# Graph products of a stack of graph-network layers: from 64 x 128 blocks of weights to 64 x 64 blocks on TensorE

## The chip, the cores and the metric

The kernel runs on one core of one Trainium2 chip. The metric is the device time of one launch in microseconds (us), as the median of several runs. A profile is one execution of the same program with the hardware profiler on; its rows name the engines PE (TensorE's matmuls), PEld (TensorE's weight loads), DVE (VectorE), ACT (ScalarE), POOL (GpSimd) and SP (SyncE, which here issues most DMAs).

## The reference

The input is `x`, 128 graphs of 64 nodes with 256 features, and one 64 x 64 adjacency matrix `adj`. Everything is fp32. Four layers follow each other; between them the stack adds the layer's input back and normalizes. Cut to what matters here:

```python
# layer 0: x <- LN(x + L0(x, adj))
agg = einsum('nm,bmd->bnd', A_hat, features)          # graph product
h   = relu(batchnorm(agg @ W1.T + b1)); out = batchnorm(h @ W2.T + b2)
# layer 1: a Laplacian product, then masked attention and an MLP
xp  = einsum('mn,bnf->bmf', L_norm, x)                # graph product
x1  = relu(layernorm(xp @ Wc + bc)) + x
q, k, v = x1 @ Wq, x1 @ Wk, x1 @ Wv                   # 4 heads of 64
o   = softmax(where(adj > 0, q k^T / 8, -1e9)) v
x2  = layernorm(x1 + o @ Wo); x = layernorm(x2 + gelu(x2 @ W1 + b1) @ W2 + b2)
# layer 2: two graph convolutions, then LSTMs over windows of 1, 2, 3 and 4 nodes
h = relu(einsum('ts,bsh->bth', adj, x @ Wg0 + bg0))   # graph product
h = relu(einsum('ts,bsh->bth', adj, h @ Wg1 + bg1))   # graph product
for p in (1, 2, 3, 4): h[last node of each window of p] = lstm_last(h windows)
# layer 3: attention with additive scores over the graph
out = softmax(mask(leaky_relu(Wh a1 + (Wh a2)^T))) Wh
```

So there are four graph products of a 64 x 64 matrix with the 64 nodes of each graph: one in layer 0, one in layer 1, two in layer 2.

## The kernel before

**Tiling.** The 128 graphs are cut into 16 blocks of 8. A block in "token-major" form is a tile of 128 partitions: partition = two graphs of 64 nodes, and beside it `NT` = 4 such pairs `t` with 256 features each. The two partition halves are `halves = slice(0, 64), slice(64, 128)`, one graph in each. In "feature-major" form the partition is one of 128 features, and the tile has two feature halves `c` with 512 tokens each.

**The graph product.** `aggregate(ps, y, mT)` (L333 to L346; its matmuls are profiled at L340) multiplies the graphs of a block with a 64 x 64 matrix that lies twice on the diagonal of `mT`. It takes the block itself as weights, so that the result comes out feature-major and needs no transpose. For each feature half `c` (2), pair `t` (4) and partition half `s` (2) there is one matmul with weights of 64 rows x 128 columns (`y[h, t, c * P : (c + 1) * P]`) and a moving operand of 64 rows x 64 columns (`mT[h, h]`). That is 16 matmuls a block, each of which the profile shows as two loads and two matmul instructions. The results for the two partition halves go to different halves of the PSUM buffer (`part(ps, s, g)`), and the copy that empties it puts them back side by side (`joined`, `runs`).

It is called for layer 0 in `first_block` (matrix `AhT`, emptied by VectorE at L574), for layer 1 in `block` (`LnT`, emptied by ScalarE at L765) and twice for layer 2 in `gcn_block` (`bdAT`, emptied by ScalarE at L1323 and L1342): 4 x 16 = 64 products.

**Neighbours on TensorE.** `to_fm` (L354) and `to_tm` (L361) transpose between the two forms with 64-row pieces, 16 to a block; the attention weights are transposed in the same way at L870. The scores of layer 1 (L836) and attention times values (L884) are matmuls of 64 x 64 weights on a 64 x 64 moving operand, 32 to a block. Full-array products with weights are `mm_fm` (L367), `mm_tm` (L379), the LSTM's (L1062, L1134, L1271, L1273), the MLP's second product (L945), and those of the second half of layer 0 (L642).

**What sets the order.** The program's order is written by a planner in the kernel itself. Every task (a block of a layer, an LSTM unit) is a generator that yields `step(engine, us, ps=..., sl=...)`: the engine of the next piece, the planner's cost for it in us, and how many PSUM buffers and SBUF tiles it takes or gives back. `flow` keeps one list of running tasks and always issues the step that can begin soonest by its own clock (with 2 us of head start for TensorE steps, `MARGIN`); there are four PSUM buffers (`PS`) and eight tiles and more that are lent later (`mem`). Each engine then executes its own queue strictly in the order issued. The costs hence change no instruction, but they decide the order on all queues, and with it which buffer a step gets and when a DMA is issued on SP.

The first `flow` runs layer 0: `first_block` for all blocks beside the chain `eig` (26 squarings of a 128 x 128 matrix for the Laplacian's largest eigenvalue, L499), then the batch norm's coefficients, then `second_block`. The second `flow` runs everything else as streams: `end_block` and `block` of layer 1, `gcn_block` of layer 2 with the first LSTM, the LSTM units of 2, 3 and 4 nodes (`unit`), and `last_block` for layer 3.

Of the kernel before, what the change touches and what calls it, by code (L numbers as in the profile page):

```python
# [15 lines left out]
P = 128  # L16
B, N, D = 128, 64, 256
NBLK = 16
TB = 512
NT = 4  # L20
# [13 lines left out]
def kernel(ctx: ExitStack, tc: tile.TileContext, a: dict, out: bass.AP):  # L34
    nc = tc.nc
    V, S, G, T = nc.vector, nc.scalar, nc.gpsimd, nc.tensor
# [206 lines left out]
    halves = slice(0, N), slice(N, P)  # L243
    for s in range(2):
        h = halves[s]
# [71 lines left out]

    def part(ps, s, g):  # L320

        return ps[:, s * TB + g * N : s * TB + (g + 1) * N]

    def joined(ps, n=2 * NT):

        return ps.rearrange("p (s g e) -> p g s e", s=2, e=N)[:, :n]

    def runs(ap):

        if len(ap.shape) == 2:  # L330
            return ap.rearrange("p (g s e) -> p g s e", s=2, e=N)
        return ap.rearrange("p t (c s e) -> p (t c) s e", s=2, e=N)

    def aggregate(ps, y, mT):


        for c in range(2):
            for t in range(NT):
                for s, h in enumerate(halves):
                    T.matmul(  # L340
                        part(ps, s, c * NT + t),
                        y[h, t, c * P : (c + 1) * P],
                        mT[h, h],
                        start=True,
                        stop=True,
                    )  # L346

    def to_fm(ps, y):

# [13 lines left out]
    def mm_fm(ps, w, yT, nk, off=0):  # L363

        for c in range(2):
            for k in range(nk):
                T.matmul(  # L367
                    ps[:, c, :],
                    w[:, k, (off + c) * P : (off + c + 1) * P],
                    yT[:, k, :],  # L370
                    start=(k == 0),
                    stop=(k == nk - 1),
                )
# [34 lines left out]
    with c0:  # L408
# [151 lines left out]
        def first_block(i):  # L560
            if i >= len(early):
                yield step("Q", 6.0, sl=1)
                xs = mem.take()
                nc.sync.dma_start(tm(mem[xs]), x_blk[i])
            else:
                xs = early[i]
            yield step("T", 0.95, ps=1, sl=1)
            ps = PS.take()
            ag = mem.take()
            aggregate(PS[ps], tm(mem[xs]), AhT)  # L570
            mem.give(xs)
            yield step("V", 1.25, ps=-1)
            aggT = fm(mem[ag])
            V.tensor_copy(runs(mem[ag]), joined(PS[ps]))  # L574
            PS.give(ps)
            for hf in range(2):
                dst = fm(Xs[i]) if hf == 0 else H[i]
                yield step("T", 3.45, ps=1)
                ps = PS.take()
                mm_fm(fm(PS[ps]), W1T, aggT, 2, off=2 * hf)  # L580
                if hf:
                    mem.give(ag)
                yield step("S", 1.3, ps=-1, waits=hf == 1)
                for c in range(2):
                    f = 2 * hf + c
                    S.activation(dst[:, c, :], fm(PS[ps])[:, c, :], AF.Identity, bias=cols["b1"][:, f : f + 1])
                PS.give(ps)
                yield step("V", 1.25, waits=hf == 1)
                for c in range(2):
                    V.bn_stats(st1[:, 2 * hf + c, i, :], dst[:, c, :])  # L590
            mark("l0a", i)
# [144 lines left out]
    def end_block(i):  # L736
        x = X[i]
        yield step("Q", 6.0, sl=1)
        xin = mem.take()
        nc.sync.dma_start(tm(mem[xin]), x_blk[i])  # L740
        yield step("S", 1.4)
        for c in range(2):
            S.activation(
                H[i][:, c, :], H[i][:, c, :], AF.Identity, scale=sc2[:, c : c + 1], bias=sh2[:, c : c + 1]
            )
        yield step("T", 0.5, ps=1)
        ps = PS.take()
        to_tm(PS[ps], H[i])
        mark("h", i)
        yield step("V", 1.25, ps=-1)  # L750
        V.tensor_tensor(runs(x), joined(PS[ps]), runs(mem[xin]), ALU.add)
        PS.give(ps)
        mem.give(xin)
        yield from ln_steps_act(x)
        mark("end", i)

    def block(i):
        x = X[i]
        mark("begun", i)
        yield step("T", 0.95, ps=1, sl=1)  # L760
        ps = PS.take()
        s_xp = mem.take()
        aggregate(PS[ps], x, LnT)
# [4 lines left out]
        ps = PS.take()  # L768
# [4 lines left out]
        y = tm(mem[s_y])  # L773
# [3 lines left out]
        yield step("V", 1.25)  # L777
        V.scalar_tensor_tensor(y, y, 0.0, x, ALU.max, ALU.add)

        yield step("T", 0.5, ps=1, sl=1)  # L780
        ps = PS.take()
        s_x1 = mem.take()
        to_fm(PS[ps], y)
# [5 lines left out]
        for w in (Wq, Wk):  # L789
            yield step("T", 3.45, ps=1, sl=1)  # L790
            ps = PS.take()
# [12 lines left out]
        ps = PS.take()  # L804
        s_v = mem.take()
        pv = PS[ps].rearrange("p (b u e) -> p b u e", b=8, u=2)
        for b in range(8):
            for r in range(2):
                for k in range(2):
# [4 lines left out]
                        start=(k == 0),  # L814
                        stop=(k == 1),
# [8 lines left out]
        G.tensor_tensor(y, y, row["bo"], ALU.add)  # L824


        yield step("T", 1.8, ps=1, sl=1)
        ps = PS.take()
        s_e = mem.take()
        pq = PS[ps].rearrange("p (r g m) -> p r g m", r=2, g=8)  # L830
        for t in range(NT):
            for u in range(2):
                for s in range(2):
                    b = 2 * t + s
                    for r in range(2):
# [4 lines left out]
                            start=True,  # L840
                            stop=True,
# [20 lines left out]
        G.tensor_tensor(em, em, bc_last(sums, N), ALU.mult)  # L862


        yield step("T", 0.5, ps=1, sl=1)
        ps = PS.take()
        s_a = mem.take()
        for g in range(8):
# [4 lines left out]
        aT = mem[s_a].rearrange("p (g m) -> p g m", g=8)  # L873
        S.copy(runs(mem[s_a]), joined(PS[ps]))
        PS.give(ps)
        yield step("T", 1.3, ps=1, sl=1)
        ps = PS.take()
        s_o = mem.take()
        po = fm(PS[ps])
        for b in range(8):  # L880
            t, s = b // 2, b % 2
            for u in range(2):
                for r in range(2):
# [4 lines left out]
                        start=True,  # L888
                        stop=True,
# [7 lines left out]
        ps = PS.take()  # L897
# [5 lines left out]
        yield from ln_steps(y)  # L903


        yield step("T", 0.5, ps=1, sl=1)
        ps = PS.take()
        s_x2 = mem.take()
        to_fm(PS[ps], y)
# [15 lines left out]
        for hf in range(2):  # L925
            yield step("T", 3.45, ps=1, sl=1)
            ps = PS.take()
# [5 lines left out]
            for c in range(2):  # L933
                f = 2 * hf + c
# [7 lines left out]
        ps = PS.take()  # L942
        for t in range(NT):
            for k in range(4):
# [4 lines left out]
                    start=(k == 0),  # L949
                    stop=(k == 3),  # L950
# [360 lines left out]
        mem.give(s_cell)  # L1311

    def gcn_block(i):
        yield step("T", 0.95, ps=1, sl=1)
        ps = PS.take()
        s_a = mem.take()
        aggregate(PS[ps], X[i], bdAT)
        yield step("Q", 4.0, waits=False)
        nc.sync.dma_start(XD[i], X[i])
        mem.add([Xs[i]], Clock.end, part=("x", i // 2) if i < 8 else None)  # L1320
        mark("x", i)
        yield step("S", 1.05, ps=-1)
        S.copy(runs(mem[s_a]), joined(PS[ps]))  # L1323
        PS.give(ps)
        yield step("T", 3.45, ps=1, sl=1)
        ps = PS.take()
        s_h1 = mem.take()
        mm_tm(tm(PS[ps]), fm(mem[s_a]), Wg0, 2)
        mem.give(s_a)
        yield step("V", 1.25, ps=-1)  # L1330
        h1 = tm(mem[s_h1])
        V.tensor_tensor(h1, tm(PS[ps]), bc_mid(rb0, NT), ALU.add)
        PS.give(ps)
        yield step("S", 1.05)
        S.activation(mem[s_h1], mem[s_h1], AF.Relu)
        yield step("T", 0.95, ps=1, sl=1)
        ps = PS.take()
        s_a = mem.take()
        aggregate(PS[ps], h1, bdAT)
        mem.give(s_h1)  # L1340
        yield step("S", 1.05, ps=-1)
        S.copy(runs(mem[s_a]), joined(PS[ps]))  # L1342
        PS.give(ps)
        yield step("T", 3.45, ps=1, sl=1)
        ps = PS.take()
        s_h2 = mem.take()
        mm_fm(fm(PS[ps]), Wg1, fm(mem[s_a]), 2)
        mem.give(s_a)
# [24 lines left out]
        mark("p", 1, i)  # L1373
# [89 lines left out]
    def last_block(i, t0=0, nt=NT):  # L1463
# [5 lines left out]
        r = nt / NT  # L1469
# [3 lines left out]
        for c in range(2):  # L1473
# [1 line left out]
                hb[:, c, :].rearrange("p (b n) -> p b n", n=N),  # L1475
                hT_block(i)[:, c, :, 2 * t0 : 2 * (t0 + nt)].rearrange("p n b -> p b n"),
            )
        yield step("T", 0.5 * r, ps=1)
        ps = PS.take()
        to_tm(PS[ps], hb)  # L1480
        mem.give(s_h)
# [3 lines left out]
        PS.give(ps)  # L1485
        yield from ln_steps_act(x)

        yield step("T", 0.5 * r, ps=1, sl=1)
        ps = PS.take()
        s_xT = mem.take()  # L1490
        to_fm(PS[ps], x)
# [11 lines left out]
        for t in range(0, nt, 2):  # L1503
            end = t == nt - 2
            yield step("T", 1.75, ps=1, sl=int(t == 0))
            ps = PS.take()
# [4 lines left out]
            for j in range(2):  # L1511
                for k in range(2):
# [4 lines left out]
                        start=(k == 0),  # L1517
                        stop=(k == 1),
# [16 lines left out]
        ps = PS.take()  # L1535
# [19 lines left out]
        ps = PS.take()  # L1555
# [8 lines left out]
        ps = PS.take()  # L1564
        po = PS[ps].rearrange("p (e u d) -> p e u d", e=2, u=2)
        for t in range(0, nt, 2):
            for j in range(2):
                for h in range(2):
# [4 lines left out]
                        start=True,  # L1573
                        stop=True,
# [170 lines left out]
```

## Time and profile before

| | |
|---|---|
| median of 3 runs | 2440.89 us (2439.8 to 2445.77) |
| profiled execution, its time | 2446.48 us |
| profiled execution, its span (first to last instruction) | 2444.7 us |
| mean granted TensorE clock | 0.979 |
| instructions | 38027 |
| DMA | 57.74 MB, 24 GB/s over the span |

How to read the rows: a group's row has the line, engine and operation, what is written and read, the shapes and how often, then busy time, mean ns of one, and the idle time just before it with what ended it. Busy time of a group is the time in which at least one of its instructions ran: instructions overlap, so a mean of 272 ns does not mean that one starts every 272 ns. For the pace of a run of matmuls the timeline is used, from the start of one row to the start of the next. A timeline row has start, length, engine, line, operation and count. Weights are shown as rows*columns ahead of the moving shape: `64*128 64x64` is 64 x 128 weights and 64 columns that move.

### The profile page before, as it was taken

To read this page: it belongs to the slowest core of one execution; us is meant where nothing else is said; L and a number is where in the kernel's file an instruction comes from. 1 tells how busy PE (TensorE), PEld (TensorE's weight loads), DVE (VectorE), ACT (ScalarE), POOL (GpSimd) and SP (SyncE) were. 2 spreads that over 40 slices of the span, in tenths; PEclk is the share of its full clock that TensorE was granted. 3 is DMA by queue.
4 is the path that set the end of the run, shared out by engine and by line. 5 is a ranking of instruction groups with operands and counts; after the bars stand their busy time and mean duration, and the time that the engine had idled before them with its cause. 6 is when DMAs were issued, how large, how long until landed. Compare 5 with 4: busy or idle time off the path is not lost. (4 is left out here: it accounts for less than half of the span.)

```text
span 2444.7 us, 38027 instructions
## 1 busy us (share of the span) xinstructions
PE 2323.0 (95%) x15636; PEld 1789.4 (73%) x15636; DVE 1255.6 (51%) x2904; ACT 1185.4 (48%) x2168; POOL 591.0 (24%) x441
## 2 busy tenths in 40 slices
PE   8999878999999999999999999999999999989997
PEld 5548655767666667566677888899999888877775
DVE  4557577656447538266334344344444445455445
ACT  1248553444444343444444444444445554567676
POOL 0002134323224223233222222222221222122112
PEclk9999889999999999999999999999999999999998
DMA  5100301100000000001000000000001000101101
GB/s 154 52 1 1 106 26 40 36 9 10 1 10 10 18 10 10 1 18 44 9 27 1 27 18 1 1 18 1 1 1 35 1 10 9 35 27 44 52 18 53
DMA packets 42622, 57.74 MB, mean 24 GB/s; under 512 B 6224, under 2 KB 35536, under 8 KB 42448
## 3 DMA queue, kind: packets, MB, share of 16 engines
q1 hardware_dynamic: 41344, 54.22, 6.8%
q8 instruction: 123, 2.02, 0.4%
q10 hardware_dynamic: 1104, 1.08, 0.1%
q14 instruction: 51, 0.42, 0.1%
HBM read 38.52 MB, written 16.78 MB: 23 GB/s over the span
## 5 line engine op out<-in xcount | busy, mean ns | idle before, releaser
L1134 PE MATMUL ps<-x,x 128*128 128x256 f32 x864 | 212.9, 381 | 1.6 <-DVE x L1193 1.0
L1134 PEld LDWEIGHTS ps<-x,x 128*128 128x128 f32 x864 | 160.6, 190 | 25.2 <-issue 2.0
L1134 PE MATMUL ps<-t,x 128*128 128x256 f32 x704 | 170.0, 380 | 0.0
L314 ACT ACTIVATE x<-x,ln_nm,ln_rs 128x256 f32<-128x256 f32 x188 | 99.6, 592 | 122.9 <-DVE ln_nm L311 122.9
L1134 PEld LDWEIGHTS ps<-t,x 128*128 128x128 f32 x704 | 132.9, 190 | 18.9 <-issue 0.8
L308 POOL TENSOR_TENSOR ln_rs<-ln_rs,neghalf 128x4 f32<-128x4 f32 (+1 forms) x72 | 69.9, 970 | 213.0 <-DVE ln_rs L274 200.7
L367 PE MATMUL ps<-t,W1T 128*128 128x512 f32 x256 | 116.5, 603 | 0.0
L1210 ACT ACTIVATE t<-t,bih 128x512 f32<-128x512 f32 (+2 forms) x63 | 40.4, 641 | 105.7 <-DVE t L1200 101.0
L294 POOL TENSOR_TENSOR ln_rs<-ln_rs,neghalf 128x4 f32<-128x4 f32 x32 | 36.6, 1143 | 224.4 <-DVE ln_rs L274 224.4
L1062 PE MATMUL ps<-h,wL 128*128 128x192 f32 (+2 forms) x456 | 90.4, 352 | 0.0
L1062 PE MATMUL ps<-h,x 128*128 128x256 f32 x384 | 86.8, 380 | 1.5 <-ACT t L1074 1.5
L1193 DVE COPY t<-ps 128x256 f32<-128x256 f32 (+2 forms) x63 | 23.4, 371 | 123.9 <-PE ps L1134 123.9
L272 DVE BATCH_NORM_STATS2 ln_st<-x 128x6 f32<-128x256 f32 x224 | 85.4, 403 | 0.4
L367 PEld LDWEIGHTS ps<-t,W1T 128*128 128x128 f32 x256 | 47.4, 194 | 49.4 <-issue 49.4
L1062 PEld LDWEIGHTS ps<-h,wL 128*128 128x128 f32 x456 | 70.1, 190 | 16.8 <-issue 15.8
L1062 PEld LDWEIGHTS ps<-h,x 128*128 128x128 f32 x384 | 72.7, 190 | 12.3 <-ACT t L1074 1.6
L1074 ACT ACTIVATE t<-ps,bih 128x512 f32<-128x512 f32 (+3 forms) x108 | 63.6, 639 | 34.3 <-PE ps L1062 34.2
L1062 PE MATMUL ps<-t,wL 128*128 128x512 f32 x168 | 73.7, 594 | 1.3 <-ACT t L1360 0.7
L1074 ACT ACTIVATE x<-ps,bih 128x512 f32<-128x512 f32 (+3 forms) x84 | 48.9, 634 | 52.3 <-PE ps L1062 52.1
L273 DVE BATCH_NORM_AGGREGATE ln_mv<-ln_st 128x2 f32<-128x6 f32 x448 | 71.6, 167 | 0.0
L1210 ACT ACTIVATE x<-x,bih 128x512 f32<-128x512 f32 (+2 forms) x64 | 41.8, 653 | 57.6 <-DVE x L1200 57.4
L1062 PE MATMUL ps<-x,wL 128*128 128x512 f32 x144 | 62.9, 593 | 0.0
(712 smaller groups left out, 5760.6 us busy)
## 6 DMA issues: line engine op xcount, KB each, us to landing
t<-in_x_dram SPq DMA_DIRECT2D x26, 512.0 KB, 4.2
xd<-x SPq DMA_DIRECT2D x16, 512.0 KB, 2.6
x<-xd SPq DMA_DIRECT2D x6, 512.0 KB, 3.4
out_dram<-x SPq DMA_DIRECT2D x6, 512.0 KB, 3.0
h<-in_x_dram SPq DMA_DIRECT2D x5, 512.0 KB, 3.9
wL<-in_L_gnn_Wih_dram SPq DMA_DIRECT2D x2, 1024.0 KB, 5.1
x<-in_L_gnn_Whh_dram SPq DMA_DIRECT2D x2, 1024.0 KB, 6.2
t<-xd SPq DMA_DIRECT2D x4, 512.0 KB, 3.6
```

What stands on the lines that cost most here:

```text
L272: V.bn_stats(st[:, t, :], y[:, t, :])
L273: V.bn_aggr(mv[:, t, :], st[:, t, :])
L294: G.tensor_tensor(rs, rs, neghalf[:, :NT], ALU.pow)
L308: G.tensor_tensor(rs, rs, neghalf[:, :n], ALU.pow)
L314: S.activation(y[:, t, :], y[:, t, :], AF.Identity, scale=rs[:, t : t + 1], bias=nm[:, t : t + 1])
L367: T.matmul(ps[:, c, :], w[:, k, (off + c) * P : (off + c + 1) * P], yT[:, k, :], start=(k == 0), stop=(k == nk - 1),)
L1062: T.matmul(spread(fm(PS[ps])[:, j, :n], q), WL[p][0][:, k, m], x_of(0, q)[:, k], start=(k == 0), stop=(k == 1),)
L1074: S.activation(of(sl)[:, j], fm(PS[ps])[:, j, :n], AF.Tanh if g == 2 else AF.Sigmoid, bias=bias(g, c))
L1134: T.matmul(dst, WS[p][name](k, g), y[:, k], start=first and k == 0, stop=k == 1, skip_group_check=not first)
L1193: V.tensor_copy(y[:, 1, :], v[:, 0, :])
L1210: S.activation(of(act[g])[:, 0], of(act[g])[:, 0], f, bias=bias(g, 0))
```

## The change

`aggregate` splits each weight block of 128 feature columns in two of 64 (`f`), and writes each to its own half of the output partitions (`[to]`). A block then takes 32 matmuls of 64 x 64 weights in the place of 16 of 64 x 128. The loop runs over the two column halves and, inside, over the two partition halves, so that four matmuls in a row use the four different quarters of the array. What is computed, where it lands and who empties it stay as they were. Beside that, the planner's costs of TensorE steps are rewritten: products, transposes, scores, attention times values, and the transposes of the last blocks. Line numbers after it stand two higher.

```diff
         for c in range(2):
             for t in range(NT):
-                for s, h in enumerate(halves):
-                    T.matmul(
-                        part(ps, s, c * NT + t),
-                        y[h, t, c * P : (c + 1) * P],
-                        mT[h, h],
-                        start=True,
-                        stop=True,
-                    )
+                for f, to in enumerate(halves):
+                    for s, h in enumerate(halves):
+                        T.matmul(
+                            part(ps, s, c * NT + t)[to],
+                            y[h, t, c * P + f * N : c * P + (f + 1) * N],
+                            mT[h, h],
+                            start=True,
+                            stop=True,
+                        )
...
# first_block, block, gcn_block (twice): ahead of aggregate
-            yield step("T", 0.95, ps=1, sl=1)
+            yield step("T", 1.15, ps=1, sl=1)
...
# end_block: to_tm; block: to_fm (twice) and the transposes of the attention weights
-        yield step("T", 0.5, ps=1)
+        yield step("T", 0.65, ps=1)
...
# block: scores
-        yield step("T", 1.8, ps=1, sl=1)
+        yield step("T", 1.15, ps=1, sl=1)
...
# block: attention times values
-        yield step("T", 1.3, ps=1, sl=1)
+        yield step("T", 1.15, ps=1, sl=1)
...
# last_block: to_tm and to_fm, r = 1 for a whole block and 0.5 for half of one
-        yield step("T", 0.5 * r, ps=1)
+        yield step("T", 0.2 + 0.45 * r, ps=1)
```

More of the change, by code (lines that the diff above doesn't have):

```diff
@@ L759, in block @@
         mark("begun", i)
-        yield step("T", 0.95, ps=1, sl=1)
+        yield step("T", 1.15, ps=1, sl=1)
         ps = PS.take()
@@ L778, in block @@
         V.scalar_tensor_tensor(y, y, 0.0, x, ALU.max, ALU.add)
-        yield step("T", 0.5, ps=1, sl=1)
+        yield step("T", 0.65, ps=1, sl=1)
         ps = PS.take()
@@ L862, in block @@
         G.tensor_tensor(em, em, bc_last(sums, N), ALU.mult)
-        yield step("T", 0.5, ps=1, sl=1)
+        yield step("T", 0.65, ps=1, sl=1)
         ps = PS.take()
@@ L875, in block @@
         PS.give(ps)
-        yield step("T", 1.3, ps=1, sl=1)
+        yield step("T", 1.15, ps=1, sl=1)
         ps = PS.take()
@@ L903, in block @@
         yield from ln_steps(y)
-        yield step("T", 0.5, ps=1, sl=1)
+        yield step("T", 0.65, ps=1, sl=1)
         ps = PS.take()
@@ L1313, in gcn_block @@
     def gcn_block(i):
-        yield step("T", 0.95, ps=1, sl=1)
+        yield step("T", 1.15, ps=1, sl=1)
         ps = PS.take()
@@ L1335, in gcn_block @@
         S.activation(mem[s_h1], mem[s_h1], AF.Relu)
-        yield step("T", 0.95, ps=1, sl=1)
+        yield step("T", 1.15, ps=1, sl=1)
         ps = PS.take()
@@ L1486, in last_block @@
         yield from ln_steps_act(x)
-        yield step("T", 0.5 * r, ps=1, sl=1)
+        yield step("T", 0.2 + 0.45 * r, ps=1, sl=1)
         ps = PS.take()
```

## Prediction

> **What bounds the kernel now.** I read the page first: busy shares, then the forty slices.
>
> ```profile
> PE 2323.0 (95%) x15636; PEld 1789.4 (73%) x15636; DVE 1255.6 (51%) x2904; ACT 1185.4 (48%) x2168; POOL 591.0 (24%) x441
> PE   8999878999999999999999999999999999989997
> PEclk9999889999999999999999999999999999999998
> ```
>
> TensorE is busy 2323 of 2444.7 us and every other compute engine is near half. A mean over stages proves little, so next comes the table of busy time in six stretches that I cut where the kind of work changes: first blocks, second blocks, ramp of layer 1, layer 1 with the graph layer, LSTM, end. Columns: stretch, length, PE, PEld, DVE, ACT, POOL busy, clock, DMA.
>
> ```profile
> 0.00:140.00 140.00, 131.96 (x781) 82.29 (x782) 69.05 (x144) 31.63 (x49) 2.51 (x15) 1.00 0.32 90
> 140.00:260.00 120.00, 113.53 (x436) 82.40 (x435) 76.48 (x136) 81.45 (x144) 22.60 (x16) 0.97 0.02 5
> 260.00:430.00 170.00, 139.81 (x1275) 101.46 (x1274) 118.36 (x307) 88.03 (x132) 54.38 (x39) 0.87 0.19 58
> 430.00:1400.00 970.00, 941.68 (x7157) 648.25 (x7156) 504.34 (x1102) 421.28 (x567) 280.15 (x173) 0.99 0.04 15
> 1400.00:2000.00 600.00, 595.30 (x3375) 540.37 (x3374) 268.74 (x544) 285.60 (x649) 139.79 (x105) 1.00 0.03 9
> 2000.00:2445.00 445.00, 400.75 (x2620) 334.59 (x2618) 218.64 (x673) 277.42 (x630) 91.61 (x94) 0.97 0.10 33
> ```
>
> PE is the bound in every stretch but two: the ramp (30 us idle) and the end (44 us idle). From 430 to 1400 it idles 28 us in 970, and in the first 140 us only 8, of which 7.5 pass before its first matmul. So PE time taken out there moves the end, unless something new holds PE up.
>
> Where are the products that change? The same table for L340 alone (PE, PEld):
>
> ```profile
> 0.00:140.00 140.00, 35.72 (x512) 34.24 (x512) 1.00 0.32 90
> 260.00:430.00 170.00, 11.35 (x128) 10.94 (x128) 0.87 0.19 58
> 430.00:1400.00 970.00, 86.74 (x1408) 81.55 (x1408) 0.99 0.04 15
> ```
>
> 2048 instructions, 64 products of 32 (each fp32 matmul is two), 16 in the first stretch, 4 in the ramp, 44 in the long PE-bound one. PEld is as busy as PE: each load of 64 x 128 weights serves a moving operand of only 64 columns.
>
> **The change part by part.** *The product itself.* Its price is read from start to next start in the timeline of PE, since the printed length holds a tail that overlaps the next row:
>
> ```profile
> 456.53 2.00 PE L340 MATMUL ps<-bdAT,t 64*128 64x64 f32 x32
> 458.36 1.95 PE L340 MATMUL ps<-bdAT,x 64*128 64x64 f32 x32
> 460.15 1.95 PE L340 MATMUL ps<-LnT,x 64*128 64x64 f32 x32
> 462.03 2.41 PE L367 MATMUL ps<-x,Wg 128*128 128x512 f32 x5
> ```
>
> 1.79 to 1.83 us when a product of the same form follows, 1.88 before a full-array one (1.93 at 1379.40). For the new form the kernel already holds a twin: the scores at L836 are 32 fp32 matmuls, so 64 instructions, of 64 x 64 weights on a moving 64 x 64, in the same order of quarters (both row halves for one column half, then the other), the row halves to different halves of the PSUM buffer.
>
> ```profile
> 330.10 1.16 PE L836 MATMUL ps<-h,t 64*64 64x64 f32 x64 [0.40 <-ACT h L820]
> 331.19 0.71 PE L354 MATMUL ps<-ident,t 64*128 64x64 f32 x15
> ...
> 1115.19 1.16 PE L836 MATMUL ps<-x,x 64*64 64x64 f32 x64
> 1116.17 1.11 PE L884 MATMUL ps<-t,t 64*64 64x64 f32 x64
> 1117.21 2.00 PE L340 MATMUL ps<-bdAT,t 64*128 64x64 f32 x32
> ```
>
> 1.09 us before another form, 0.98 before its own: 0.11 is the price of changing the array's form behind it. The built order of the changed kernel has 51 of the 64 products followed by another form (41 before, because the transposes had the old form), so about 1.08 us on average against 1.87: **0.79 us less each**. Before the product, 48 enter from another form against 46: nothing.
>
> The Trainium skill speaks against this: "TensorE: Matmul & The Clock Gate", in the section "Wait — 56ns, not 53.3ns?", says that matmul starts never come closer than about 25 ns, however small the matmul. Twice as many instructions would then take 64 x 25 = 1.6 us, saving 0.27 each and 17 us in all. The row gives 1.09 us for 64, or 17 ns a start, under that floor; the row decides. A skill-based sum would be 2424.
>
> *Clock.* Five products ran at about half pace: three between 9.32 and 20.68 (3.5 us each) and two at 289 to 296 (3.6), where the granted clock reads 0.50. At half pace the new form should take twice 1.08, so 1.4 less each. The first three are only worth half: L367's matmuls go from 0.86 to 0.43 us apart at about 25 us, and if that moment stays put, slow work fills the gap. Sum: 59 x 0.79 = 46.6; three at 0.7 = 2.1; two at 1.4 = 2.8; together **51.5 us of PE**.
>
> *What of it lies beside other work.* In the ramp PE waits for LN and copies, and I strike half of the two warm products there: -0.8. In the 970 us the other engines' work is squeezed into 935, and waits of PE that were hidden come out: between 0 and a doubling of the 28 us idle; I take 3, as DVE goes only from 52% to 54%. In the first stretch each product is copied out by DVE in 1.22 us (L574), more than the new 1.08; a run of products then goes at DVE's pace, but at most three stand together and buffers lie between: -0.3.
>
> *The step costs.* The change also rewrites what the planner thinks of steps: products 0.95 to 1.15, transposes 0.5 to 0.65, scores 1.8 to 1.15, attention times values 1.3 to 1.15, and the same for the last blocks. These issue nothing. But the planner writes every queue's order from them, so all five queues are reordered (SP's loads and stores too: layer-3 reads and output stores change places). Instruction counts are equal apart from the products and ACT's table loads, 78 before, 68 after: 10 x 1.28 us of ACT, half of them among layer 1's gelu and exp, where ACT is 43% busy and hides them; at most 2 us reach PE. The new costs stand closer to the rows (1.15 for 1.09, where 0.95 stood for 1.87), which should not hurt. No row prices an order; I bound it by the places where PE idles and could idle less or more: about a third of the 102 us idle in ramp, long stretch and end, so -30 to +30, and take 0, since the order's shape at the end is nearly the same: behind the last LSTM matmul of L1134 stands about 154 us of PE work (151 before), priced by shape. DMA is busy 3 to 10% after 430 us, and hides any moved transfer; without that cover a 512 KB read costs 3.4 us.
>
> Sum: 51.5 - 0.8 - 3 - 0.3 = 47.4, and about 0.5 for the table loads: **48 us**. The profiled execution took 2446.5 us (span 2444.7), so 2398.5; it was 5.6 above the median of the runs, 2440.9, so the median to expect is **2393**.
>
> **The rivals.**
>
> *A, the waits shrink too.* Better costs give a better order; a third of the 102 us is won: 2393 - 25 = about 2368 to 2378. For: before, 64 products were planned at half their length, so PE ran late against the plan. Against: of the 28 us idle, the named waits are single events of 1 to 3.5 us.
>
> *B, evacuation takes over.* "TensorEngine Tiling (Array Packing)", section "PSUM Bottleneck", says tiling quickens TensorE but not the emptying of PSUM. ACT's copy behind a product takes 1.01 us (L765, L1323), DVE's 1.22; neither shrinks. If every product had its copy exposed by a third, 64 x 0.35 = 22 back: 2415. Against: ACT waited for these copies, not the reverse (L1323 15.7 and 13.7 us for L340), and four PSUM buffers with other streams' matmuls lie between.
>
> *C, slower: the end comes apart.* From 2000 us PE already idles 44 of 445 us waiting for ACT and DVE in LSTM gates and last blocks. If the new order puts the last LSTM units so late that last blocks stand alone behind them, PE idle there grows. It decides once the added idle passes 48 + 7 = 55 us, more than a doubling: say 70 added, 2463. Against: the 154 against 151 us above.
>
> *D, the quarters don't run side by side.* One matmul after another at the old 57 ns would make 64 x 57 = 3.65 us a product and cost 64 x 1.8 = 114 us: 2555; break-even is at 29 ns a start. The twin at 17 ns nearly excludes it; the only difference is that two quarters here read the same moving operand.
>
> **How the numbers follow.** The forecast has 0.66, A 0.16, B 0.13, C 0.04, D 0.01. The forecast's own range is 2380 to 2406 (half of the order's and waits' bounds). The range for 8 in 10 takes in most of A and B: 2371 to 2412. A measurement tells about 0.3%, 7 us, from no change. Faster than that: forecast, A and nearly all of B, 0.94; within it, B's far end, 0.02; slower, C and D with some room for an order that I can't price, 0.04.
>
> **What would show it.** Right: L342 (the moved L340) with 4096 PE instructions and about 75 us busy against 134; the product from start to next start 0.98 to 1.10 us; PE busy near 2270; idle in 430 to about 1365 at 25 to 35 us; the end of the graph-layer stretch some 45 us earlier. Wrong: 25 ns a start (the skill's floor) or more; L574 or the ACT copies in the list of PE's waits with over 10 us; more than 70 us idle in the last 445 us (C); PE idle in the long stretch doubled.

## The result and the profile after

The changed kernel takes 2427.91 us (median of four runs, 2427.06 to 2429.18) against 2440.35 us for the kernel before on the same chip: a ratio of 0.9945, 95% interval 0.9928 to 0.9962. That is faster, by 12.4 us or half a per cent. The forecast said 48, and its wider range, for 8 in 10, ended at 2412.

The page of the changed kernel: busy time, then the forty slices of PE and its clock.

```profile
PE 2278.0 (94%) x17684; PEld 1741.2 (72%) x17684; DVE 1257.5 (52%) x2904; ACT 1174.4 (48%) x2158; POOL 592.9 (24%) x441
PE   7999798989999999999999999999999999998995
PEclk9999798999999999999999999999999999999997
```

PE is busy 45.0 us less (2323.0 before), but the span, 2425.5, is only 19.2 shorter than the 2444.7 of before, whose profiled run was 5.6 above its own median. The rest is idle time of PE: 2425.5 - 2278.0 = 147.5 us against 121.7. The same six stretches as before show where. Columns: stretch, length, PE, PEld, DVE, ACT, POOL busy, clock, DMA.

```profile
0.00:140.00 140.00, 126.33 (x1319) 69.75 (x1320) 72.15 (x154) 35.47 (x55) 2.52 (x15) 0.98 0.34 91
140.00:260.00 120.00, 113.49 (x461) 86.81 (x459) 76.34 (x134) 80.68 (x145) 22.41 (x16) 0.97 0.05 14
260.00:430.00 170.00, 135.96 (x1454) 95.80 (x1454) 118.32 (x313) 86.05 (x126) 56.09 (x40) 0.86 0.19 55
430.00:1400.00 970.00, 927.33 (x8535) 624.00 (x8534) 516.44 (x1110) 423.11 (x577) 287.42 (x175) 0.98 0.05 16
1400.00:2000.00 600.00, 595.96 (x3424) 546.59 (x3423) 265.28 (x536) 280.64 (x649) 140.80 (x105) 1.00 0.02 7
2000.00:2425.00 425.00, 378.94 (x2499) 318.26 (x2497) 208.99 (x663) 268.44 (x608) 83.67 (x91) 0.95 0.10 34
```

The stretch that held 28 us of PE idle now holds 970 - 927.3 = 42.7; the first holds 13.7 (8.0), the ramp 34.0 (30.2). The LSTM stretch is unchanged, as is the end (46.1 against 44.3).

Was the product itself as cheap as forecast? The same table for its matmuls alone (L342, which was L340), and two places of PE's timeline:

```profile
0.00:140.00 140.00, 18.78 (x1024) 17.28 (x1024) 0.98 0.34 91
260.00:430.00 170.00, 8.80 (x320) 7.22 (x320) 0.86 0.19 55
430.00:1400.00 970.00, 50.85 (x2752) 44.84 (x2752) 0.98 0.05 16
```

```profile
61.31 1.16 PE L342 MATMUL ps<-AhT,t 64*64 64x64 f32 x64
62.40 0.49 PE L501 MATMUL ps<-eM 128*128 128x128 f32 x2
...
98.10 2.09 PE L342 MATMUL ps<-AhT,t 64*64 64x64 f32 x128
100.12 0.49 PE L501 MATMUL ps<-eM 128*128 128x128 f32 x2
```

Yes. Twice the instructions take 78.4 us in all where 133.8 stood. From start to next start a product takes 1.09 us, two in a row 2.02: 16 to 17 ns a matmul on average. So 55 us of TensorE work is gone (54 by 64 products at 0.84 us, below), and the question is who took back 43 of them. The list of PE's waits (columns: waiting line, what it waited for, us in total, times, longest) begins so:

```profile
PE ps L356 <- ACT x L314: 6.8, 1, 6.8
PE ps L501 <- DVE eM L505: 6.7, 2, 6.1
...
PE ps L947 <- ACT t L937: 6.0, 2, 3.2
...
PE ps L369 <- ACT x L788: 4.5, 1, 4.5
PE ps L947 <- ACT x L937: 4.3, 1, 4.3
PE ps L947 <- ACT h L937: 4.0, 1, 4.0
```

Four of the rows left out (PE waiting at L472, L363 and L610, and at L356 for L780: 5.0 to 6.4 us each) stand in the list of before too, as long or longer. No wait is large and few repeat, and no copy behind a product is among the leaders: normalization (L314), gelu (L937), copies ahead of the next projection. There is no one thief, so the experiments separate three suspects: the new order, the chains between the matmuls, and GpSimd.

### The profile page after: what moved, and what is told of

It is laid out like the page before. It is cut to its first block, busy times and chain, and to the rows that moved or that the text cites. A ratio compares the mean times of both kernels' runs of the same rounds, so it can differ in the third digit from the quotient of the medians.

```text
span 2425.5 us, 42138 instructions
## 1 busy us (share of the span) xinstructions
PE 2278.0 (94%) x17684; PEld 1741.2 (72%) x17684; DVE 1257.5 (52%) x2904; ACT 1174.4 (48%) x2158; POOL 592.9 (24%) x441
## 5 line engine op out<-in xcount | busy, mean ns | idle before, releaser
L1136 PE MATMUL ps<-x,x 128*128 128x256 f32 x896 | 220.0, 380 | 0.8 <-DVE x L1204 0.7
L1136 PEld LDWEIGHTS ps<-x,x 128*128 128x128 f32 x896 | 167.0, 190 | 22.2 <-DVE x L1204 0.9
L314 ACT ACTIVATE x<-x,ln_nm,ln_rs 128x256 f32<-128x256 f32 x172 | 91.3, 592 | 121.2 <-DVE ln_nm L311 121.2
L369 PE MATMUL ps<-t,W1T 128*128 128x512 f32 x256 | 117.6, 606 | 0.0
L1064 PE MATMUL ps<-h,wL 128*128 128x192 f32 (+2 forms) x480 | 101.0, 364 | 0.0
L1076 ACT ACTIVATE t<-ps,bih 128x512 f32<-128x512 f32 (+3 forms) x116 | 69.7, 652 | 37.2 <-PE ps L1064 36.9
L369 PEld LDWEIGHTS ps<-t,W1T 128*128 128x128 f32 x256 | 47.5, 194 | 49.5 <-issue 49.4
L1064 PEld LDWEIGHTS ps<-h,x 128*128 128x128 f32 x384 | 72.5, 190 | 11.9 <-DVE h L903 1.3
L272 DVE BATCH_NORM_STATS2 ln_st<-x 128x6 f32<-128x256 f32 x208 | 79.8, 404 | 0.4
L369 PE MATMUL ps<-t,wA 128*128 128x512 f32 x144 | 70.1, 633 | 2.5 <-ACT t L788 2.5
L1136 PE MATMUL ps<-x,wA 128*128 128x192 f32 (+1 forms) x352 | 65.5, 313 | 1.1 <-DVE t L1204 1.1
L1202 DVE TENSOR_TENSOR t<-ps,t 128x512 f32<-128x512 f32 (+2 forms) x61 | 36.7, 602 | 56.0 <-PE ps L1136 47.0
```

Source lines behind the costliest of these rows:

```text
L272: V.bn_stats(st[:, t, :], y[:, t, :])
L314: S.activation(y[:, t, :], y[:, t, :], AF.Identity, scale=rs[:, t : t + 1], bias=nm[:, t : t + 1])
L369: T.matmul(ps[:, c, :], w[:, k, (off + c) * P : (off + c + 1) * P], yT[:, k, :], start=(k == 0), stop=(k == nk - 1),)
L1064: T.matmul(spread(fm(PS[ps])[:, j, :n], q), WL[p][0][:, k, m], x_of(0, q)[:, k], start=(k == 0), stop=(k == 1),)
L1076: S.activation(of(sl)[:, j], fm(PS[ps])[:, j, :n], AF.Tanh if g == 2 else AF.Sigmoid, bias=bias(g, c))
L1136: T.matmul(dst, WS[p][name](k, g), y[:, k], start=first and k == 0, stop=k == 1, skip_group_check=not first)
```

## The experiments

Medians and ratios are against the kernel before, run beside them. "Idle" is the span less PE's busy time.

One thing has to be added to the kernel's description: the built queues are not quite the planner's list. Instructions of one engine can change places (GpSimd runs L434, L436, L435, L437 in e3), and two L361 transposes stand inside a product of before at 294.05 us. "Same order" below is that of the built queues.

**The two halves of the change alone.** First, quarters with all the planner's costs as before; the built order is then the one of before but for a handful of neighbours that changed places (8 of PE's other 13588 instructions, 14 of DVE's 2904, 4 of ACT's 2168):

```diff
# e1: from the changed kernel, all costs put back
-            yield step("T", 1.15, ps=1, sl=1)   # and every other new cost
+            yield step("T", 0.95, ps=1, sl=1)
# e2: from the changed kernel, the product put back
-                for f, to in enumerate(halves):
-                    for s, h in enumerate(halves):
-                        T.matmul(part(ps, s, c * NT + t)[to], y[h, t, c * P + f * N : c * P + (f + 1) * N], ...)
+                for s, h in enumerate(halves):
+                    T.matmul(part(ps, s, c * NT + t), y[h, t, c * P : (c + 1) * P], ...)
```

> The product in quarters, every step cost of the planner as before: the built order of all queues is then that of the kernel before but for a handful of transposes. Theory 'order' (the new costs wrote an order with more idle PE): about 2400 us, the 48 us of the forecast less some 8 us for the stall at the start, where VectorE sits behind the sums of layer 0's second weights; PE idle near 125 us and busy near 2275. Theory 'squeeze' (with less PE work the same chains on ACT, DVE and POOL show, whatever the order): 2422 to 2432 us, PE idle 145 us or more.

> The old product (64 x 128 weights), all new step costs: the order of the changed kernel with the old PE work. Theory 'order': slower than before by about the 25 to 30 us that the changed kernel lacks, 2465 us. Theory 'squeeze': 2441 us within 6, as the longer products cover the chains again.

e1: 2420.08 us, ratio 0.9914 (0.9897 to 0.9931), idle 144.4. e2: 2457.62 us, 1.0074 (1.0055 to 1.0093). So the new costs lose 17 us with the old product and 8 with the new one, and they are the smaller part: with the order kept, the quarters bring 20.7 us, not 54. Both results lie between what the two theories named, e1 just under the range of "squeeze".

Because e1 has before's order, its matmuls can be compared one by one, and the lead (start in before less start in e1) drawn up along the run. It was 10.9 us at 138 us behind 16 products, 17.8 at 436 behind 21, and 26.9 at 1400 behind all 64. Up to 436 us nothing is missing: 21 x 0.84 = 17.6. Behind that it is a staircase. Nearly every product lifts the lead by 0.74 to 0.95 us, typically 0.84, and in between it falls. Summed over the matmuls between 440 and 1420 us, where the interval to the matmul before grew: 17.8 us fell in single intervals above 1.3 us (waits), and 13.1 us in short ones, nearly all runs of matmuls at half pace (L367 at 0.85 us instead of 0.43, L379 at 0.43 instead of 0.22) behind a wait. Against both stand 43 products, 36 us, and 4.7 of other gains, mostly half-pace runs of before that are gone. The granted clock says the same: its mean over this stretch is 0.990 in before and 0.981 in e1 (422 to 1393 us there). (5.6 us of the lead at the end is before's own profiled run above its median.)

Sixteen idle times just before a matmul grew by more than 0.15 us there, by 15.6 us together. 11.9 of it came at ten places where PE of before had already waited, 0.4 to 3.5 us each. A result of ScalarE ended twelve of the sixteen; copies behind a product (L1324, L1343) are 2.0 us of it.

The largest fall, 6.2 us, reads off the timelines of all engines. Before:

```profile
598.23 1.38 DVE L285 TENSOR_SCALAR h<-h,ln_mv,ln_rs 128x256 f32<-128x256 f32 x4 [1.19 <-POOL ln_rs L282]
599.52 1.28 DVE L1352 TENSOR_TENSOR t<-ps,rb 128x512 f32<-128x512 f32 x2
600.60 0.71 PE L354 MATMUL ps<-ident,h 64*128 64x64 f32 x16
...
600.89 1.06 ACT L1360 ACTIVATE t<-t 128x1024 f32<-128x1024 f32 x1 [9.64 <-DVE t L1352]
601.40 2.36 POOL L824 TENSOR_TENSOR h<-h,rows 128x1024 f32<-128x1024 f32 x1 [3.21 <-PE ps L354]
...
602.01 1.55 PE L1062 MATMUL ps<-t,wL 128*128 128x512 f32 x3 [0.70 <-ACT t L1360]
```

And e1, lines one higher:

```profile
576.72 0.71 PE L355 MATMUL ps<-ident,h 64*128 64x64 f32 x16
576.81 3.40 DVE L285 TENSOR_SCALAR h<-h,ln_mv,ln_rs 128x256 f32<-128x256 f32 x4 [1.20 <-POOL ln_rs L282]
577.53 2.54 POOL L825 TENSOR_TENSOR h<-h,rows 128x1024 f32<-128x1024 f32 x1 [0.75 <-PE ps L355]
580.13 1.27 DVE L1353 TENSOR_TENSOR t<-ps,rb 128x512 f32<-128x512 f32 x2
...
581.50 1.06 ACT L1361 ACTIVATE t<-t 128x1024 f32<-128x1024 f32 x1 [14.10 <-DVE t L1353]
...
582.61 1.22 PE L1063 MATMUL ps<-t,wL 128*128 128x512 f32 x1 [5.17 <-ACT t L1361]
```

Follow the bracket of each row backwards. The LSTM's matmul waits for ACT, ACT for DVE's add, and that stands in DVE's queue behind L285, which waited for GpSimd's L282: a chain that the product is not part of, and which the earlier PE only waits on for longer. And a second thing: the transposes came 2.5 us earlier relative to L285, so GpSimd's add, released by them, now runs beside L285, whose four instructions take 3.40 us instead of 1.38. The faster engine started what slowed its own supplier. After the 5.17 us wait the next four intervals between matmuls are 1.01 to 0.78 us instead of 0.53 to 0.43. The granted clock (third number from the right) is 0.50 there, where before had 1.00; first e1, then before:

```profile
582.60:584.60 2.00, 1.99 (x3) 0.95 (x4) 0.00 (x0) 2.00 (x3) 0.00 (x0) 0.50 0.00 0
```

```profile
602.00:604.00 2.00, 1.99 (x5) 1.04 (x6) 0.00 (x0) 2.00 (x3) 1.76 (x1) 1.00 0.00 0
```

**Is PE the bound at all?** The old product, issued twice, so that PE gets work and nobody else:

```diff
-                for s, h in enumerate(halves):
-                    T.matmul(part(ps, s, c * NT + t), y[h, t, c * P : (c + 1) * P], ...)
+                for _ in range(2):
+                    for s, h in enumerate(halves):
+                        T.matmul(part(ps, s, c * NT + t), y[h, t, c * P : (c + 1) * P], ...)
```

> The kernel before with every product issued twice into the same place (32 matmuls of 64 x 128 weights), costs and order as before: 64 x 1.8 = 115 us more of PE. If PE is the bound nearly everywhere, as the forecast had it, 2540 to 2556 us. If products weigh 0.4 of their length in both directions (the 20.7 us for 50.2 us of the run with the old costs), 2487 us. Theory 'squeeze', where other engines' chains stand just behind PE: adding weighs more than taking away, 0.7 to 0.9 of it, 2520 to 2545 us, with PE idle falling below 110 us.

2540.60 us, 1.0388 (1.0367 to 1.0409): PE's busy time rises by 115.1 us and the time by 97.6 (the kernel before beside it: 2443.03), so 0.85 of what is added is paid, and idle falls to 103.1. The time lies in the ranges of two theories at once; the idle under 110 speaks for "squeeze". Of what e1 takes away (50.2 us of PE busy) 20.7 come out, 0.41. The kernel before stood about where PE stops being the only bound: over steps of this size, a microsecond more costs nearly one, and one less brings less than half of one.

**GpSimd beside VectorE.** Four adds and multiplies on whole blocks left out (`bo`, `g2`, `b2`, `be3`: 64 instructions of 2.35 us), their steps left in the plan:

```diff
-        G.tensor_tensor(y, y, row["bo"], ALU.add)
...
-        G.tensor_tensor(y, y, row["g2"], ALU.mult)
-        G.tensor_tensor(y, y, row["b2"], ALU.add)
...
-        G.tensor_tensor(x, x, row["be3"], ALU.add)
# e6: from e1; e9: from the kernel before; e11: from the changed kernel
```

> Quarters with the old costs (2420 us) without GpSimd's four elementwise steps of a layer 1 block (adding bo, b2 and be3, multiplying by g2: left out of the computation); the built order of PE and DVE is the same. In that trace a DVE normalization (L285) took 3.4 us in the place of 1.4 beside such a step, and PE then waited 5.2 us. If that meeting of GpSimd and VectorE is a main part of what is lost: L285 back at 1.4 us, PE idle down by 8 us or more, 2400 to 2412 us. If it is one accident among many waits: 2416 to 2420 us.

> The kernel before (halves, old costs) without the same four GpSimd steps of a layer 1 block; PE and DVE orders as before. With the quarters this computation took 2373.7 us. Theory 'squeeze through VectorE and GpSimd' (the product's gain is lost because VectorE, slowed by GpSimd, stands just behind PE): without those steps the product is worth nearly its PE time, 45 to 50 us, so 2419 to 2424 us here. If the gain is lost elsewhere, the product is worth 21 us here too: 2394 us.

> The changed kernel (quarters, new costs, 2428 us) without those four steps. If what the new order costs (8 us here, 17 with halves) is only how GpSimd's steps happen to meet VectorE's: within 5 us of the old order's 2373.7, so 2369 to 2379 us. If the new order is worse in itself: 2381 us or more.

| | with the 64 steps | without | difference |
|---|---|---|---|
| halves, old costs | 2440.4 | 2407.78, ratio 0.9856 (0.9840 to 0.9871) | 33 |
| quarters, old costs (e1, e6) | 2420.08 | 2373.67, ratio 0.9710 (0.9694 to 0.9726) | 46 |
| quarters, new costs | 2427.91 | 2398.20, ratio 0.9814 (0.9796 to 0.9832) | 30 |

In the same order on PE and DVE the quarters are worth 20.7 us with these steps and 34.1 without. So about 13 of the 33 us missing from 54 come back, while about 20 stay missing: e6 fell below both of its ranges, and e9's 2407.8 lies between its two theories. (The kernel before beside these runs had medians of 2440.4 to 2445.5 us; taken from the ratios the quarters are worth 21 and 36 us, so 15 come back.) The new costs lose 8 us with these steps and 25 without (2373.7 to 2398.2), so what that order costs is not the way GpSimd's steps meet VectorE's. Matched as above between 440 and 1420 us, e6 against e9 loses 10.8 us in waits and 3.7 at half pace, where e1 against before lost 17.8 and 13.1.

The steps have no product in them and DVE keeps its 2904 instructions, yet its busy time falls by 51.4 us. The page's first lines of e1 and of e6:

```profile
PE 2272.8 (94%) x17684; PEld 1733.1 (72%) x17684; DVE 1256.3 (52%) x2904; ACT 1184.8 (49%) x2168; POOL 592.3 (25%) x441
```

```profile
PE 2257.5 (95%) x17684; PEld 1727.6 (73%) x17684; DVE 1204.9 (51%) x2904; ACT 1185.6 (50%) x2168; POOL 436.1 (18%) x377
```

Why shows in the minimum, median and maximum (ns) of L285, in e1 and in e6:

```profile
L285 DVE TENSOR_SCALAR t<-t,ln_mv,ln_rs x36: 379/407/2436, 355.3 to 1270.7; 128x256 f32<-128x256 f32 x36
```

```profile
L285 DVE TENSOR_SCALAR t<-t,ln_mv,ln_rs x36: 381/407/415, 354.6 to 1225.7; 128x256 f32<-128x256 f32 x36
```

And one chain with two meetings, first in e1 and then in e6. PE stood at 354.54 us in both just before:

```profile
355.28 2.35 POOL L825 TENSOR_TENSOR t<-t,rows 128x1024 f32<-128x1024 f32 x1
355.35 3.40 DVE L285 TENSOR_SCALAR t<-t,ln_mv,ln_rs 128x256 f32<-128x256 f32 x4
...
362.80 2.34 POOL L923 TENSOR_TENSOR t<-t,rows 128x1024 f32<-128x1024 f32 x1
362.87 2.29 DVE L311 SCALAR_TENSOR_TENSOR ln_nm<-ln_mv,ln_rs 128x4 f32<-128x4 f32 x1 [1.19 <-POOL ln_rs L308]
365.08 1.21 DVE L902 TENSOR_TENSOR t<-ps,t 128x1024 f32<-128x1024 f32 x1
...
366.35 1.22 PE L368 MATMUL ps<-h,wA 128*128 128x512 f32 x1 [5.96 <-DVE t L902]
```

```profile
354.60 1.38 DVE L285 TENSOR_SCALAR t<-t,ln_mv,ln_rs 128x256 f32<-128x256 f32 x4
...
360.09 0.16 DVE L311 SCALAR_TENSOR_TENSOR ln_nm<-ln_mv,ln_rs 128x4 f32<-128x4 f32 x1 [1.19 <-POOL ln_rs L308]
360.17 1.22 DVE L901 TENSOR_TENSOR t<-ps,t 128x1024 f32<-128x1024 f32 x1
...
361.45 1.13 PE L368 MATMUL ps<-h,wA 128*128 128x512 f32 x2 [1.50 <-DVE t L901]
```

A DVE instruction on 4 columns takes 2.29 us in the place of 0.16: GpSimd's L923, one of the steps left out in e6, began 0.07 us before it, and both end together. Ahead of it four L285 take 3.40 us instead of 1.38 beside L825, again begun 0.07 us before. The wait of PE is 5.96 us with the steps and 1.50 without; of the 4.46 between, the two meetings are 2.02 and 2.13. Two limits of this reading. Dropping the steps also shortens the chains that contain them; a variant in which GpSimd does the same work on a tile that nobody needs was not tried, so how the 46 us divide between meetings and dependencies stays open. And the quarters did not make meetings more frequent as a whole: instructions of L274, L285, L297, L300 and L311 above 0.7 us number 35 before and 36 in e1. So GpSimd lengthens some of the chains that the faster product then runs into.

**The start.** In the changed kernel PE meets a wait that before did not have. Two engines' rows, in order of time:

```profile
11.92 1.16 PE L342 MATMUL ps<-AhT,t 64*64 64x64 f32 x64
...
16.66 0.42 DVE L434 TENSOR_TENSOR wB<-W2T 128x256 f32<-128x256 f32 x1 [5.16 <-DMA W2T<-in_L_gnn_W_dram]
...
18.81 0.28 DVE L505 COPY eM<-ps 128x128 f32<-128x128 f32 x1
...
19.14 0.80 PE L501 MATMUL ps<-eM 128*128 128x128 f32 x2 [6.06 <-DVE eM L505]
```

DVE stands at the head of its queue for a load of weights that nothing needs yet, PE's next operand is behind it, and afterwards eight L369 matmuls take 6.08 us where the same eight take 3.60 later on (the granted clock is 0.50 from 19.1 to 23 us). So the sums of W2T go to GpSimd, with its own cost:

```diff
-            yield step("V", 1.7)
+            yield step("G", 3.4)
-            V.tensor_tensor(W2S[0], a21, a22, ALU.add)   # and the other three
+            G.tensor_tensor(W2S[0], a21, a22, ALU.add)
```

> The changed kernel, with the four sums of layer 0's second weights on GpSimd in the place of VectorE: its queue then no longer holds the copy for the next squaring while those weights are on their way. If that stall (6.1 us of idle PE up to 19.1 us, and 2.5 us at half pace behind it) is a real loss, the first stretch ends 8 us earlier and the time is 2419 to 2421 us. If another wait (the loads of x or W1) takes its place, 2426 to 2428 us.

2425.49 us, 0.9933 (0.9918 to 0.9947): nothing that counts. The stall went, and PE ran on to the next of its kind, DVE's L730, which waits for a load of `be`:

```profile
36.58 0.80 PE L501 MATMUL ps<-eM 128*128 128x128 f32 x2 [4.55 <-DVE eM L505]
```

The first statistics of layer 0 were gathered at 150.2 us, as in the changed kernel (150.6; 161.6 before). The start had lost little in the first place: 11.0 us of the 12.4 forecast for its products were there.

**The order.** First the product's cost alone is changed, then the scores' and attention's costs are put back, and then only the planner's head start:

```diff
# e4: from e1
-            yield step("T", 0.95, ps=1, sl=1)   # the four products
+            yield step("T", 1.15, ps=1, sl=1)
# e13: from the changed kernel; scores, and attention times values
-        yield step("T", 1.15, ps=1, sl=1)
+        yield step("T", 1.8, ps=1, sl=1)        # 1.3 for the latter
# e8: from e4
-MARGIN = {"T": 2.0, "V": 0.5, "S": 0.5}
+MARGIN = {"T": 3.0, "V": 0.5, "S": 0.5}
```

> The product in quarters with its own cost raised from 0.95 to 1.15 and all other step costs as before: a third order. Theory 'order': it falls apart from the changed kernel by more than noise, anywhere in 2395 to 2440 us, with the PE idle time going along with it. Theory 'squeeze': 2422 to 2432 us like the changed kernel.

> The changed kernel (2428 us) with the old costs of scores (1.8) and attention times values (1.3). Raising the product's cost alone gave 2409, all costs 2428. If the lower cost of the scores is what makes the order worse (it lets the planner put less before their use): back to 2405 to 2415 us, and PE's waits for the gelu's results (ACT L937) gone. If the draw is luck: anywhere in 2405 to 2440 us, not nearer to 2409 than to 2428 by rule.

> The same kernel with 3 us in the place of 2 us of head start for PE steps in the planner: another order, with more time between a result and its use. Theory 'order' (luck of the draw): anywhere in 2400 to 2430 us. Theory 'squeeze' (results come too late for PE): more distance helps, PE idle under 125 us and 2395 to 2405 us.

e4: 2409.28 us, 0.9868 (0.9853 to 0.9882), idle 131.8. e13: 2410.26 us, 0.9859 (0.9842 to 0.9876), idle 138.9; PE's waits for gelu at L947 fall from 14.3 us to 9.6. e8: 2440.47 us, 0.9990 (0.9982 to 0.9997), idle 152.5, outside what either theory named. From e4 and e13 one would say that the truer cost of the product is worth 11 us and that the scores' cost does harm. Both may read a cause into one draw, that is, into one of the many orders that the planner could have written. Two costs that mean nothing test it:

```diff
# e14 and e15: from the changed kernel, the four products
-            yield step("T", 1.15, ps=1, sl=1)
+            yield step("T", 1.10, ps=1, sl=1)   # e15: 1.20
```

> The changed kernel with 1.10 in the place of 1.15 as the product's cost, nothing else: a change of the plan that means nothing (1.08 is measured). If the order's effect follows from what the costs say: 2428 within 4 us. If it is the luck of a draw: off by 5 to 15 us either way.

> The same with 1.20. If the order's effect follows from what the costs say: 2428 within 4 us. If it is the luck of a draw: off by 5 to 15 us either way, and not the mirror image of 1.10.

2425.23 us (0.9921, 0.9905 to 0.9937) and 2447.83 us (1.0022, 1.0015 to 1.0030). Down by 0.05 us, the time moves by 3 us, hardly more than noise; up by 0.05, it is 20 us longer, with the same instructions on PE; idle goes from 147.5 to 166.8. The list of e15's waits begins:

```profile
PE ps L356 <- DVE x L285: 7.9, 1, 7.9
PE ps L472 <- DVE etmp L470: 7.1, 1, 7.1
PE ps L356 <- ACT x L314: 6.8, 1, 6.8
PE ps L356 <- DVE x L753: 6.5, 1, 6.5
```

The first and the fourth, 14.4 us, are not in the changed kernel's list at all.

Seven orders with the new product thus lie between 2409 and 2448 us; the changed kernel's is the fifth of them. Of the old product only two are on record (2440 and 2458), so how far its orders spread stays open.

**A better version.** The start again, from e4, with both loads that DVE stood waiting for:

```diff
# the W2T sums as in e3, and
-        V.tensor_tensor(rb2, rb2, be2, ALU.add)
+        G.tensor_tensor(rb2, rb2, be2, ALU.add)
```

> The kernel with the product's cost alone raised (2409 us), with both of VectorE's early steps that wait for a load (the sums of layer 0's second weights, and b2 + be2) moved to GpSimd. With the sums alone the stall only moved to the second of them (4.6 us at 36.6 us). If the loads in DVE's queue are all that holds PE there: no PE wait over 1 us between 8 and 140 us, the first batch norm some 8 us earlier, 2400 to 2403 us. If a third wait takes over: 2407 to 2410 us.

2399.67 us (2398.68 to 2401.14), 0.9817 (0.9801 to 0.9833): the fastest of the kernels that leave nothing out, 9.6 us under e4 and 28 under the changed kernel. Between 8 and 140 us no wait of PE is over 0.6 us now (4.6 in e4), and the first statistics of layer 0 come at 142.8 us instead of 150.9: 8.1 of the 9.6 us show up there. Last, from it, one normalization is applied by ScalarE, to take meetings away from DVE:

```diff
-        yield from ln_steps(y)
+        yield from ln_steps_act(y)
```

> The kernel of 2399.7 us (quarters, product's cost alone raised, early loads on GpSimd) with the normalization ahead of the MLP applied by ScalarE in the place of VectorE: 64 instructions of 0.41 us and their stretched cases leave VectorE, 64 of 0.59 us come to ScalarE, and the order is drawn anew. Theory 'squeeze through VectorE and GpSimd': VectorE is relieved where it is slowed, 2385 to 2398 us. If ScalarE, which releases most of PE's waits, is as near: 2400 to 2415 us.

2414.64 us, 0.9881 (0.9865 to 0.9896): 15 us slower than e7, though DVE's busy time falls from 1240.8 to 1218.4. A redrawn order and a longer chain through ACT cannot be told apart here.

## Why the prediction was wrong

**The product: right.** 0.79 us each was forecast, 0.84 is the usual step in the matched order; L342 is busy 78.4 us where about 75 was named. The twin at L836 was the right row to take. The floor of 25 ns in the Trainium skill ("TensorE: Matmul & The Clock Gate", "Wait — 56ns, not 53.3ns?") would give 1.6 us for 64; the trace has 1.09, and the row was rightly preferred. That the sum made with the floor, 2424, lies beside the result is luck.

**"Waits of PE that were hidden come out ... I take 3": the step that failed.** In before's own order it is about 31 us between 440 and 1420 us: 17.8 of longer waits, 13.1 of matmuls at half pace behind them; 26 are left when the 4.7 of other gains are taken off. The bound of the term (a doubling of the 28 us idle) was set by the idle there was. But an idle of 0.7 or 2 us is not slack that runs out slowly; it marks a place where PE already met a chain of other engines, and there the lead won since the last such place can be handed back: 11.9 of the 15.6 us of grown idle came at such places. That DVE goes "only from 52% to 54%" was no argument: the chains DVE, GpSimd, ACT are serial, and in the first example DVE itself waited 1.2 us for GpSimd. The pace behind a wait was not in the sum at all, which counted the clock as a gain alone (4.9 us for the five slow products); the mean granted clock of the whole run fell from 0.979 to 0.970 in the changed kernel. And its sign of being wrong, idle doubled in the long stretch, could not show this: idle went from 28 to 43 us, and half pace is busy time.

**What the sum had no row for.** The price of GpSimd beside DVE was in the trace of before (L285: median 408 ns, maximum 2445), but the prediction never looked at the spread of a DVE group. The Trainium skill states the rule in "SBUF — State Buffer", section "Who interferes with whom": the two share a pair of ports under an exclusive lock; a DVE instruction with two SBUF inputs contends with a GpSimd instruction that reads SBUF, and so does a `tensor_scalar` in a 2-port mode, where the one that comes second is blocked for the whole of the other. The rows agree for L311, which reads two tensors in SBUF and ends with GpSimd's add, and for `TENSOR_TENSOR t<-ps,t`, with one input from PSUM, which keeps its 1.21 us beside one (L902 at 365.08, GpSimd's L924 at 365.22). L285 has one tensor input and is stretched all the same; that it runs in a 2-port mode no row shows: alone it takes 0.41 us, as an add of two tensors of that size does (L434, 0.42).

**"No row prices an order ... -30 to +30, and take 0":** the size was right, the value not. The new costs are worth -8 us with the new product, against what was said ("should not hurt"), and e15 warns against reading a cause into it. The whole sum: 54 won, 33 handed back, 8 lost to the order, 13 left against 12.4 measured.

**The end of the graph-layer stretch.** The last product starts at 1333.5 us instead of 1392.8, 59 earlier where some 45 were forecast, and that would have been read as success. But 38 us more of PE's busy time stand behind it now (1041.2 against 1003.3), and in before's own order (e1) it starts at 1366.1, only 27 earlier: an order moves work across a landmark. A landmark in time only tells something in a fixed order.

**The rivals.** A (waits shrink) went the other way: idle rose by 25.8 us. (A third of its 102 us would also be 34, not 25.) B's number, 2415, is nearest, but not by its mechanism: PE waits 2.2 us in all for a copy behind a product (L1344), and before had one such wait too, 3.0 us for L1323; what stood behind the product was other chains, with normalization, gelu and the copies of other steps in them. So what the section cited for B ("PSUM Bottleneck") says of PSUM's copies accounts for about 2 us here. C (the end comes apart) was not seen: 46.1 us idle in the last 425 us against 44.3 in 445. D is excluded by 17 ns a start. What the ten table loads that went (78 to 68) are worth no run tells apart from the order.

## What to carry to other kernels

Before crediting work taken off a bound engine, list its waits, however short, and treat each as a place where the gain since the last one may be handed back; doubling the work (0.85 paid here) and removing it (0.41 won) are different experiments, and only the second prices a saving. Compare a change in a fixed order first, with every planner cost left alone, and then move a cost by an amount that means nothing: here 0.05 us more of it made the time 20 us longer, more than the whole change won, so a comparison across two orders can't carry a cause alone. Look at the maxima of short instructions on one engine, not only at its busy share: an instruction that takes 0.16 us alone and 2.29 beside another engine is a dependency that no semaphore shows.

## What the runs showed of the hardware that was not expected

- Two quarters on one moving operand run as fast as two on different ones: 64 matmuls of 64 x 64 weights start 17 ns apart on average, 1.09 us for all, as the scores at L836 do.
- DVE's L285, 0.41 us alone, takes up to 2.44 us beside GpSimd's 2.35 us add; leaving 64 such adds and multiplies out takes 51.4 us from DVE's busy time (e6 against e1).
- A wait of a few microseconds costs PE again behind it: eight L369 matmuls took 6.08 us instead of 3.60 after a wait of 6.06, with the granted clock at 0.50, and in matched order half-pace matmuls were 13.1 of the 31 us handed back.
